# Cross-attention with prompts: value columns of the even batches moved from SyncE's DMA queue to GpSimd's and ScalarE's

## The chip, the cores and the metric

The kernel runs on one core of a Trainium2 chip. A core has TensorE (PE), VectorE (DVE), ScalarE (ACT) and GpSimd (POOL) for arithmetic. DMA transfers are issued in the instruction streams of SyncE (SP), ScalarE and GpSimd, and each stream is worked off in order. The metric is the device time of one execution in microseconds (us), the median of several runs; less is better.

## The reference

For each of 8 batches, 112 queries of 320 channels attend over 375 context tokens of 512 channels, with 20 heads of 16 channels. The last 4 tokens are image prompts with weights of their own; the other 371 are text.

```python
q, k_t, v_t = heads(hidden @ W_q), heads(text @ W_k), heads(text @ W_v)
probs_t  = softmax(q k_t^T * scale)                    # 112 x 371 for each head
text_out = probs_t @ v_t
qsem = l2norm(probs_t @ text)                          # 512 channels for each query and head
sem  = qsem @ l2norm(ip)^T                             # 4 prompts
probs_ip = softmax(q k_ip^T * scale + 0.5 * sem) * spatial_mask
out = (text_out + probs_ip @ v_ip) @ W_out + b_out + hidden
```

## The kernel before, in words

**One product for each head.** The norm of `probs_t @ text` needs only the Gram matrix of the text tokens. So the kernel multiplies the probabilities of each head with a tile `u`, whose columns are the Gram matrix of the context (symmetric, so only its upper part is held, in three chunks of 128 tokens), the prompts, a one for the sum of the probabilities, and the head's own 16 value columns. A product therefore gives the norm, the prompt similarities, the sum and the text output at once. It runs over 12 blocks of 32 tokens (`product`, L830 to L843). The 20 heads of a batch are taken as 5 groups of 4; the four heads of a group lie on four bands of 32 partitions and multiply side by side.

**How `u` comes about.** For each batch the Gram rows are computed by `gram` into `ug` and copied by 16 DMAs to the four bands of `u` (`gram_to_groups`, L543). The values are computed by `values` (L595) into `vext`: for even batches after the first, chunks 0 and 1 come from `two_chunks` (L644), whose last sums are made by GpSimd (L667), and chunk 2 is copied by ScalarE (L612). `values_to_dram` (L684) stores `vext` to a tile `vd` in DRAM, with the token bands in the order in which `u` holds them: four DMAs for chunks 0 and 1, two for chunk 2. `values_to_groups` (L704) loads it again into `vr` with the heads split over the four bands: four DMAs for each call, each to 32 partitions, in rows of 80 floats. `placed` (L751) then has GpSimd copy the 16 columns of each head of the next group from `vr` into `u`, one copy for each chunk (L755). There are two buffers of `u`, used by batches in turn; within a batch a copy must wait until PE has read the previous group's columns of that chunk.

**How the probabilities come.** PE multiplies queries and keys (L789), DVE takes the negated maximum (L802), ACT the exponential (L806), SyncE's DMAs place each head's probabilities in `xg` (L813), and DVE transposes them into the stationary operand of the product (L825). ACT also copies the prompt logits out of the score bank (L808).

**The order of the work is written out by hand.** Inside the main loop each engine's instructions stand in the order of the program. The loop takes the 40 steps (batch, group) in twos. `pair` (L1256) multiplies two groups against each other, interleaved with scores and probabilities of steps to come. In it, `placed` (L1275, L1288) has the second group's value columns put in; then comes `moved` (L1289), which issues transfers for the next batch; then pieces of `finish` (L1293 to L1295), the end of the previous batch, then `reduced` (L1296). `behind` (L1336) issues what PE does after a pair: projections, the Gram matrix and values of the next batch, and further pieces of `finish`.

**The finish of a batch** (`finish`, L907) is cut into pieces. GpSimd scales the prompt values (L973), adds them up (L976) and adds them to the attention (L980); PE turns the attention round (L985), ACT copies it (L989), and PE multiplies it with the output weights (L994).

**The stretch of the change.** For the odd batches b = 1, 3, 5 and the even batch nb = b + 1 after each, the program runs as follows. `behind` of group 1 has PE compute the values of chunks 0 and 1 of nb, and stores them. The pair of groups 2 and 3 of b follows; after the copies for group 3, `moved(b, 2)` loads chunks 0 and 1 of nb (L1334), and then `f(b - 1, 2)` issues the finish's piece with L973 to L980. `behind` of group 3 loads queries for later (L1443, issued by GpSimd at L178), computes chunk 2 of the values, turns the attention round (L985), stores chunk 2, makes keys (L563), runs the output product (L994), and moves the last Gram rows and the value columns of chunk 2 (L1451, L1452). The next pair is group 4 of b with group 0 of nb, which reads the new columns.

Of the kernel before, what the change touches and what calls it, by code (L numbers as in the profile page):

```python
# [20 lines left out]
def kernel(  # L21
# [14 lines left out]
    nc = tc.nc  # L36
# [6 lines left out]
    NT = (T + P - 1) // P  # L43
# [304 lines left out]
    def turned_inputs(bs, i0=0, i1=NC):  # L348

        t0, n = blocks_of(bs)  # L350
        if bs[0] not in inputs_turned:
            inputs_turned[bs[0]] = work.tile(
                [P, NC, 2 * S], F32, tag="xT", name=f"xT_{bs[0]}", bufs=1
            )
        xT = inputs_turned[bs[0]]
        nc.vector.transpose(
            xT[:, i0:i1, : n * RG].rearrange("p i (j r) -> p j i r", r=RG),
            x_in[:, :n, i0 * RG : i1 * RG].rearrange("p j (i c) -> p j i c", c=RG),
        )
# [53 lines left out]
    def load_next(b):  # L413
        if 2 <= b < B:
            loaded[b] = load_ctx(b)
# [127 lines left out]
    def gram_to_groups(b, blocks, eng=nc.sync):  # L543

        for q in blocks:
            for a in range(GROUP):
                eng.dma_start(
                    st[b]["u"][a * RG : (a + 1) * RG, q * GW : (q + 1) * GW],
                    ug[q * RG : (q + 1) * RG, :],
                )  # L550
# [133 lines left out]
    def values_to_dram(b, eng, c0=0, c1=NT):  # L684
        s = st[b]
        if b == 0:
            eng.dma_start(
                s["vd"][c0 * P : c1 * P].rearrange("(c p) x -> p c x", p=P),
                s["vext"][:, c0:c1, :C],
            )  # L690
            return
        for c in range(c0, c1):
            q = 0
            while q < QN:
                p, n = DEAL[c].index(q), 1
                while q + n < QN and p + n < QN and DEAL[c][p + n] == q + n:
                    n += 1
                to = c * P + p * RG
                eng.dma_start(
                    s["vd"][to : to + n * RG], s["vext"][q * RG : (q + n) * RG, c, :C]  # L700
                )
                q += n

    def values_to_groups(b, c0=0, c1=NT):  # L704
        s = st[b]
        w = NG * D
        for a in range(GROUP):
            nc.sync.dma_start(
                s["vr"][a * RG : (a + 1) * RG, c0 * QN : c1 * QN].rearrange(
                    "p j g d -> p j (g d)"  # L710
                ),
                s["vd"][c0 * P : c1 * P, a * w : (a + 1) * w].rearrange("(j i) x -> i j x", i=RG),
            )

    def prompt_values(b):

        nc.sync.dma_start(
            st[b]["vip"].rearrange("p n h d -> p (n h d)"),
            vipd[b * NIP : (b + 1) * NIP, :].rearrange("n c -> (n c)").partition_broadcast(S),
        )  # L720
# [94 lines left out]
    def transposed(b, g, j0=0, j1=BLK):  # L815

        xg = x_ring[(b * NG + g) % NX]
        if j1 < j0 + 1:
            return
        if ("xT", g) not in st[b]:  # L820
            st[b]["xT", g] = work.tile([P, BLK, P], F32, tag="xgT", name=f"xgT_{b}_{g}")
        xT = st[b]["xT", g]
        n = BLK // (2 if b == B - 1 or (b, g) == (0, 0) or j1 - j0 < BLK else 1)
        for j in range(j0, j1, n):
            nc.vector.transpose(  # L825
                xT[:, j : j + n].rearrange("p j (k q) -> p q j k", q=QN),
                xg[:, :, j * RG : (j + n) * RG].rearrange("p q (j k) -> p q j k", k=RG),
            )
# [379 lines left out]
    def f(b, pieces=1):  # L1208
        if b >= 0:
            run(("f", b), lambda: finish(b), pieces)  # L1210

    def k(b, pieces=1):
        run(("k", b), lambda: keys(b), pieces)

    def v(b, pieces=1):
        run(("v", b), lambda: values(b), pieces)

    def gr(b, pieces=1):
        run(("g", b), lambda: gram(b), pieces)
# [100 lines left out]
    def moved(b, g):  # L1320

        nb = b + 1
        if b % 2 == 0:
            if g in (1, 2):
                gram_to_groups(nb, (g - 1,))
            if g == 3:
                todo = [lambda: gram_to_groups(nb, (3,)), lambda: values_to_groups(nb)]
                for move in reversed(todo) if nb == B - 1 else todo:
                    move()
        else:  # L1330
            if g in (0, 1):
                gram_to_groups(nb, (g,))
            if g == 2:
                values_to_groups(nb, 0, 2)  # L1334

    def behind(n):  # L1336

        b, g = steps[n]
        nb = b + 1
        two = steps[n + 1 : min(n + 3, len(steps) - NG + 1)]  # L1340

        def tr(i):
            if i < len(two):
                transposed(*two[i], 0, BLK // (1 + i))

        if b % 2 == 0 and g == 0:
            if n == 0:
                turn[:] = ["sc", "sc", "mm"]
                turned_inputs(pairs[1])
            else:  # L1350
                turn[:] = ["qd"] * 4 + ["mm"]
                k(b)
                nc.scalar.preload_act_table(AF.Sqrt)
                f(b - 1)
                if b - 1 < B - 2:
                    prompt_values(b - 1)
            if n:
                token_sums(nb)
                gr(nb)
                tr(0)  # L1360
            if n:
                gr(nb, 2)
                f(b - 1)
            v(nb)
            if n == 0:
                k(nb)
                run(("pp",), prompt_projections)
            if n:
                tr(1)
                f(b - 1, 2)  # L1370
            load_next(b + 2)
        elif b % 2 == 0 and g == 2:
            turn[:] = ["qd"] * (8 if b else 3) + ["mm"]
            gram_to_groups(nb, (2,))
            if b == 0:
                run(("pp",), None)
                prompt_keys(nb)
                tr(0)
                v(nb)
                q(nb)  # L1380
                values_to_dram(nb, nc.scalar, 0, 2)
                v(nb)
                values_to_dram(nb, nc.scalar, 2)
                run(("pp",), None)
            else:
                values_to_dram(nb, nc.gpsimd, 2)
                k(nb)
                tr(0)
                v(nb)
                q(nb)  # L1390
                values_to_dram(nb, nc.gpsimd, 0, 2)
            tr(1)
        elif b % 2 == 0 and nb < B - 1:
            turn[:] = ["qd"] * (4 + (b > 0)) + ["mm", "mm"]
            turned(b + 2)
            token_sums(b + 2)
            q(nb)
            if b > 0:
                f(b - 1)
            else:  # L1400
                run(("t", b), lambda: prompt_logits(b))
            k(nb)
            tr(0)
            if b > 0:
                f(b - 1)
            gr(nb + 1, 3)
            if b > 0:
                f(b - 1)
            if n + 1 not in late:
                tr(1)  # L1410
            load_next(b + 3)
            f(b)
            prompt_values(b)
        elif b % 2 == 0:
            turn[:] = ["qd"] * 4 + ["mm"]
            q(nb, 2)
            f(b - 1)
            k(nb)
            nc.scalar.preload_act_table(AF.Sqrt)
            tr(0)  # L1420
            f(b - 1, 2)
            prompt_values(b)
            f(b, 2)
        elif g == 1:
            turn[:] = ["qd"] * 7 + ["sc", "mm", "mm"]
            gram_to_groups(nb, (2,))
            nc.scalar.preload_act_table(AF.Sqrt)
            q(b)
            k(b)
            f(b - 1)  # L1430
            nc.scalar.preload_act_table(AF.Exp)
            k(nb)
            tr(0)
            f(b - 1)
            v(nb)
            tr(1)
            f(b - 1)
            values_to_dram(nb, nc.sync, 0, 2)
            if b == B - 3:
                prompt_values_by_head()  # L1440
        else:
            turn[:] = ["qd"] * 3 + ["sc"]
            load_turned(nc.gpsimd, pairs[(b + 3) // 2])  # L1443
            v(nb)
            f(b - 1)
            values_to_dram(nb, nc.sync, 2)
            tr(0)
            k(nb)
            f(b - 1, 2)
            tr(1)  # L1450
            gram_to_groups(nb, (3,))  # L1451
            values_to_groups(nb, 2)  # L1452
        assert not turn, (b, g, turn)

    for n in range(0, len(steps) - NG, 2):
# [4 lines left out]
        b, g = steps[n]  # L1460
# [16 lines left out]
    b = B - 1  # L1477
# [125 lines left out]
```

## Time and profile before

| | |
|---|---|
| time, median of 3 runs | 407.21 us (406.81 to 408.14) |
| the profiled execution | 405.13 us |
| its span in the trace | 403.4 us |
| granted TensorE clock | 0.999 |
| busy PE, DVE, ACT, POOL | 398.0, 331.3, 198.5, 182.7 us |

The span is what the profiler saw of one execution, from the first instruction to the last; the execution took 1.7 us more. Times of the trace count from the start of the span. L755 is line 755 of the kernel. PEld is TensorE's weight load, which overlaps its matmuls (PE). "SPq" and "POOLq" are the sequencers that issue DMAs and wait for semaphores. In a name such as `u<-vr`, the left side is written and the right side is read. A timeline row gives start, length, engine, line, operation, shapes and count, and in brackets how long the engine had been idle and what released it; neighbouring instructions of one kind are merged. Matmuls are pipelined and their ends are modelled.

### The profile page before, as it was taken

The numbers are of one execution on the slowest core, as the hardware profiler recorded it, in microseconds if no ns is written. First come the engines' busy times: TensorE is split into PE (matmuls) and PEld (weight loads), VectorE is DVE, ScalarE is ACT, GpSimd is POOL, SyncE is SP. The second block draws the span as 40 slices with busy tenths as digits, with TensorE's granted clock in tenths as the row PEclk, the third lists the DMA queues.
The fourth block names the chain that finished last, engine by engine and source line by source line (L and its number), as shares of the span: only waits on it lengthen the run. The fifth ranks groups of instructions, "written<-read, shape, count | busy, mean of one in ns | idle before, by whom it ended". The sixth has DMA issues, their size and how long they took to land.

```text
span 403.4 us, 14380 instructions
## 1 busy us (share of the span) xinstructions
PE 398.0 (99%) x5673; PEld 321.9 (80%) x5673; DVE 331.3 (82%) x703; ACT 198.5 (49%) x707; POOL 182.7 (45%) x391
## 2 busy tenths in 40 slices
PE   8999999999999999999999999999999999999996
PEld 7867688888878787978787878877886878887894
DVE  3445789887998897987998898897798988888984
ACT  3146333337443943525653665334743485446764
POOL 7746021151571658051563338532256155704681
PEclk9999999999999999999999999999999999999999
DMA  7969846778666957567557766566746544776311
GB/s 228 215 186 225 189 130 179 207 190 184 166 172 166 220 130 185 148 161 166 155 157 165 199 165 171 160 171 152 187 126 174 131 124 117 195 172 174 107 52 28
DMA packets 58390, 65.85 MB, mean 163 GB/s; under 512 B 20165, under 2 KB 51641, under 8 KB 58324
## 3 DMA queue, kind: packets, MB, share of 16 engines
q1 hardware_dynamic: 54814, 58.23, 57.5%
q0 software_dynamic: 2336, 5.42, 5.4%
q10 hardware_dynamic: 1174, 1.29, 1.0%
q8 instruction: 45, 0.74, 0.9%
q14 instruction: 21, 0.17, 0.2%
HBM read 20.22 MB, written 5.22 MB: 63 GB/s over the span
## 4 chain that ended last, share of the span: by engine, by line
PE 97%; POOL 1%; DMA 1%; issue 0%; ACT 0%; SPq 0%; POOLq 0%
PE ps_qd L837 46%; PE ps_k L563 10%; PE ps_g L533 8%; PE ps_v L605 7%; PE ps_s L789 6%; PE ps_vs L663 6%; PE ps_q L394 3%; PE ps_o L994 3%; PE ps_k L580 3%; PE ps_g L495 1%; DMA ct<-in_ctx_dram 1%; PE ps_a L985 1%; PE ps_q L376 1%; PE ps_c L464 0%; POOL attn L980 0%; PE ps_o L1086 0%
## 5 line engine op out<-in xcount | busy, mean ns | idle before, releaser
L837 PE MATMUL ps_qd<-u,xgT 32*112 32x40 f32 (+11 forms) x3840 | 216.9, 352 | 0.2
L837 PEld LDWEIGHTS ps_qd<-u,xgT 32*112 32x112 f32 x3840 | 179.6, 172 | 32.0 <-issue 4.8
L825 DVE STREAM_TRANSPOSE xgT<-xg 128x768 f32<-128x768 f32 (+1 forms) x63 | 123.2, 1974 | 6.6 <-DMA xg<-p 5.9
L806 ACT ACTIVATE p<-ps_s,nmx 112x371 f32<-112x371 f32 x160 | 85.5, 585 | 63.2 <-DVE nmx L802 62.1
L802 DVE TENSOR_REDUCE nmx<-ps_s 112x1 f32<-112x371 f32 x160 | 76.7, 532 | 23.9 <-PE ps_s L789 22.5
L755 POOL COPY u<-vr 128x64 f32<-128x64 f32 x120 | 27.0, 237 | 152.4 <-PE ps_qd L837 82.8
L890 DVE CUSTOM_DVE_ANT_0 p<-ps_qd,p 112x371 f32<-112x371 f32 x152 | 73.5, 541 | 11.7 <-ACT pvs L864 7.4
L789 PE MATMUL ps_s<-kT,qm 32*112 32x375 f32 (+1 forms) x320 | 61.3, 485 | 0.0
L864 ACT COPY pvs<-ps_qd 112x21 f32<-112x21 f32 x152 | 21.8, 200 | 55.6 <-DVE ss L890 49.8
L563 PE MATMUL ps_k<-ctxT,wk_sb 128*128 128x371 f32 x128 | 43.4, 482 | 0.0
L563 PEld LDWEIGHTS ps_k<-ctxT,wk_sb 128*128 128x128 f32 x128 | 23.1, 190 | 12.8 <-issue 0.8
L533 PE MATMUL ps_g<-ctxT 128*32 128x119 f32 (+11 forms) x672 | 32.7, 338 | 0.0
L533 PEld LDWEIGHTS ps_g<-ctxT 128*32 128x32 f32 x672 | 27.7, 109 | 6.1 <-POOL xs L639 1.3
L789 PEld LDWEIGHTS ps_s<-kT,qm 32*112 32x112 f32 x320 | 27.6, 171 | 6.1 <-POOL vext L667 1.1
L605 PE MATMUL ps_v<-wv_sb,ctxT 128*128 128x320 f32 x96 | 28.3, 441 | 0.0
L452 DVE STREAM_TRANSPOSE ctxT<-ct 128x512 f32<-128x512 f32 x21 | 22.5, 1084 | 5.0 <-DMA u<-ug 5.0
L808 ACT COPY ipl<-ps_s 112x4 f32<-112x4 f32 x140 | 24.3, 174 | 0.0
L605 PEld LDWEIGHTS ps_v<-wv_sb,ctxT 128*128 128x128 f32 x96 | 17.5, 190 | 6.6
L570 ACT COPY kT<-ps_k 128x371 f32<-128x371 f32 x16 | 7.5, 469 | 23.1 <-PE ps_k L563 23.1
L973 POOL TENSOR_TENSOR vip<-vip,w 112x1280 f32<-112x1280 f32 (+1 forms) x8 | 17.5, 2185 | 0.2 <-DVE w L967 0.2
L517 POOL TENSOR_TENSOR ug<-ug,half 128x128 f32<-128x128 f32 (+1 forms) x24 | 10.6, 450 | 14.9 <-ACT ug L516 12.8
L512 ACT ACTIVATE ug<-ps_g 128x279 f32<-128x279 f32 (+5 forms) x24 | 8.0, 333 | 18.3 <-DMA ct<-in_ctx_dram 7.8
(179 smaller groups left out, 441.5 us busy)
## 6 DMA issues: line engine op xcount, KB each, us to landing
xg<-p SPq DMA_DIRECT2D x159, 162.3 KB
u<-ug SPq DMA_DIRECT2D x120, 99.0 KB
ct<-in_ctx_dram SPq DMA_DIRECT2D x28, 176.0 KB
vip<-vipd SPq DMA_DIRECT2D x7, 560.0 KB
vr<-vd SPq DMA_DIRECT2D x20, 120.0 KB
out_dram<-ob SPq DMA_DIRECT2D x7, 140.0 KB
vr<-vd SPq DMA_DIRECT2D x12, 80.0 KB
x_in<-in_x_dram POOLq DMA_DIRECT2D x12, 70.0 KB, 3.7
```

Of the source, the lines that this page charges most:

```text
L533: nc.tensor.matmul(ps[p * RG : (p + 1) * RG, s0 : T - t0], ctxT[:, e, t0 + q * RG : t0 + (q + 1) * RG], ctxT[:, e, t0 + s0 : T], start=(e ...
L563: nc.tensor.matmul(ps[:, :TT], wk_sb[:, e, i * P : (i + 1) * P], s["ctxT"][:, e, :TT], start=(e == 0), stop=(e == NE - 1),)
L605: nc.tensor.matmul(ps[:, :C], ctxT[:, e, c * P : (c + 1) * P], wv_sb[:, e, :], start=(e == 0), stop=(e == NE - 1),)
L663: nc.tensor.matmul(ps[:, :CH], a[:, k], t[:, k], start=(k == 0), stop=(k == 1))
L755: nc.gpsimd.tensor_copy(region(b, c)[:, :, UV - c * P :], s["vr"][:, c * QN : (c + 1) * QN, g, :])
L789: nc.tensor.matmul(ps[:S, :w], qm[a * RG : (a + 1) * RG, i, r, j * S : (j + 1) * S], s["kT"][a * RG : (a + 1) * RG, i, :w], start=True, st ...
L802: nc.vector.tensor_reduce(nmx, ps[:S, :TT], AX.X, ALU.max, negate=True)
L806: nc.scalar.activation(p, ps[:S, :TT], AF.Exp, bias=nmx)
L808: nc.scalar.copy(s["ipl"][:, groups[g][a], :], ps[:S, TT:T])
L825: nc.vector.transpose(xT[:, j : j + n].rearrange("p j (k q) -> p q j k", q=QN), xg[:, :, j * RG : (j + n) * RG].rearrange("p q (j k) -> p ...
L837: nc.tensor.matmul(banks[a][:S, j * RG : UW], xT[a * RG : (a + 1) * RG, j, :S], region(b, c)[a * RG : (a + 1) * RG, p, q * RG :], start=(j ...
L890: nc.vector.tensor_tensor_reduce(out=p, in0=ps[:S, :TT], in1=p, scale=1.0, scalar=0.0, op0=ALU.mult, op1=ALU.add, accum_out=s["ss"][:, h : ...
```

## The change

For the even batches 2, 4 and 6, four groups of transfers go by other queues:

- the stores of chunks 0 and 1 to DRAM: GpSimd in place of SyncE;
- the loads of chunks 0 and 1 into `vr`, issued by `moved`: GpSimd in place of SyncE;
- the store of chunk 2: ScalarE in place of SyncE;
- the loads of chunk 2: GpSimd in place of SyncE, and in the program ahead of the last Gram rows, which stay on SyncE.

The transfers themselves, their sizes and the data are the same. Batches 0, 1, 3, 5 and 7 are as they were.

```diff
-    def values_to_groups(b, c0=0, c1=NT):
+    def values_to_groups(b, c0=0, c1=NT, eng=nc.sync):
         s = st[b]
         w = NG * D
         for a in range(GROUP):
-            nc.sync.dma_start(
+            eng.dma_start(
...
             if g == 2:
-                values_to_groups(nb, 0, 2)
+                values_to_groups(nb, 0, 2, nc.gpsimd)
...
             f(b - 1)
-            values_to_dram(nb, nc.sync, 0, 2)
+            values_to_dram(nb, nc.gpsimd, 0, 2)
             if b == B - 3:
                 prompt_values_by_head()
...
             v(nb)
             f(b - 1)
-            values_to_dram(nb, nc.sync, 2)
+            values_to_dram(nb, nc.scalar, 2)
             tr(0)
             k(nb)
             f(b - 1, 2)
             tr(1)
+            values_to_groups(nb, 2, NT, nc.gpsimd)
             gram_to_groups(nb, (3,))
-            values_to_groups(nb, 2)
```

## The prediction

> **What bounds the kernel now.** I read the page first, for which engine the end hangs on, then the chain in order of time, for whether that engine ever waits near the lines of the change, and then the timelines of the engines that get the moved transfers. From the page: the granted clock in 40 slices, the chain by engine, and one group.
>
> ```profile
> PEclk9999999999999999999999999999999999999999
> ...
> PE 97%; POOL 1%; DMA 1%; issue 0%; ACT 0%; SPq 0%; POOLq 0%
> ...
> L825 DVE STREAM_TRANSPOSE xgT<-xg 128x768 f32<-128x768 f32 (+1 forms) x63 | 123.2, 1974 | 6.6 <-DMA xg<-p 5.9
> ```
>
> TensorE (PE) is 97% of the chain, at full clock in every slice. So time comes off only where PE itself waits, and whatever makes PE wait goes on the end in full, because no later idle stretch takes it up again. The whole case is then: which PE waits sit beside SyncE's transfers of the value columns, and does the new place of those transfers make PE wait?
>
> The chain in order of time (start, length, what) round the second of the three even batches that change, and the same stretch of the third:
>
> ```profile
> 209.59 2.35 PE ps_v L605 x8
> 211.95 0.29 PE ps_a L985 x3
> 212.24 2.51 PE ps_k L563 x8
> 214.75 1.61 PE ps_o L994 x6
> 216.36 1.15 PE ps_qd L837 x10
> ...
> 227.06 1.40 PE ps_k L580 x15
> ...
> 311.37 1.15 PE ps_qd L837 x10
> ...
> 322.60 0.46 PE ps_k L580 x3
> ```
>
> From 209.59 to 216.36 each piece begins where the one before ended: no gap. The product pair that follows takes 227.06 - 216.36 = 10.70 us here and 322.60 - 311.37 = 11.23 us in the third batch: 0.53 us lost there. That is what late SyncE placements cost: the weight load that sat idle in that pair is this one (PE weight loads, timeline; the bracket is idle time and its releaser).
>
> ```profile
> 317.19 1.83 PEld L837 LDWEIGHTS ps_qd<-u,xgT 32*112 32x112 f32 x34 [0.26 <-ACT ipl L808]
> ```
>
> It waited for a bank that ScalarE (ACT) empties after the scores, and ScalarE was late behind VectorE, whose transposes (L825) are on the page with 5.9 us of waiting for xg<-p. Relieving SyncE can give back this 0.53 us and little more; in the second batch the pair lost nothing.
>
> **What GpSimd is doing there.** GpSimd (POOL), timeline, second batch, contiguous rows:
>
> ```profile
> 199.47 1.50 POOL L667 TENSOR_TENSOR vext<-vext,v 128x160 f32<-128x160 f32 x3
> 202.14 0.24 POOL L755 COPY u<-vr 128x64 f32<-128x64 f32 x1 [1.17 <-PE ps_qd L837]
> 203.60 0.24 POOL L755 COPY u<-vr 128x64 f32<-128x64 f32 x1 [1.22 <-PE ps_qd L837]
> 205.14 0.25 POOL L755 COPY u<-vr 128x64 f32<-128x64 f32 x1 [1.30 <-PE ps_qd L837]
> 205.38 2.47 POOL L973 TENSOR_TENSOR vip<-vip,w 112x1280 f32<-112x1280 f32 x1
> 207.92 1.54 POOL L976 TENSOR_TENSOR vip<-vip 112x640 f32<-112x640 f32 x1
> 209.54 1.81 POOL L980 TENSOR_TENSOR attn<-attn,vip 112x320 f32<-112x320 f32 x2
> 211.29 0.59 POOL L755 COPY u<-vr 128x64 f32<-128x64 f32 x3
> 211.81 2.41 POOL L178 DMA_DIRECT2D x_in<-in_x_dram  x4
> ```
>
> The weight load of the attention transposes, PE, same batch:
>
> ```profile
> 211.51 0.51 PEld L985 LDWEIGHTS ps_a<-ident,attn 112*128 112x128 f32 x3
> ```
>
> These rows carry the forecast. From the copy at 205.14 on, GpSimd works without a pause through L973, L976 and L980; L980 ends at 209.54 + 1.81 = 211.35, and the weight load that reads its result begins at 211.51. GpSimd's part of the finish is just in time, and PE's matmul (211.95) follows at once. The first and the last of the three batches look the same:
>
> ```profile
> 114.39 1.81 POOL L980 TENSOR_TENSOR attn<-attn,vip 112x320 f32<-112x320 f32 x2
> ```
> ```profile
> 116.40 0.51 PEld L985 LDWEIGHTS ps_a<-ident,attn 112*128 112x128 f32 x3
> ```
> ```profile
> 304.55 1.81 POOL L980 TENSOR_TENSOR attn<-attn,vip 112x320 f32<-112x320 f32 x2
> ```
> ```profile
> 306.52 0.51 PEld L985 LDWEIGHTS ps_a<-ident,attn 112*128 112x128 f32 x3
> ```
>
> 116.20 against 116.40, and 306.36 against 306.52. In the code, moved(b, 2) stands between placed() (L1288, the copy at 205.14) and f(b-1, 2) (L1295, which issues L973 to L980). The change puts four loads on GpSimd exactly there.
>
> **The change, part by part.** Prices first: GpSimd's stores of this tile and their landing, and its loads of x_in, which are four transfers of 32 partitions in rows of 320 bytes like the moved loads (duration min/median/max in ns).
>
> ```profile
> L699 POOL DMA_DIRECT2D vd<-vext x18: 502/529/590, 153.2 to 351.6; - x18
> ...
> DMA to landing us min/median/max: 2.5/3.1/3.8
> ```
> ```profile
> L178 POOL DMA_DIRECT2D x_in<-in_x_dram x16: 548/592/668, 30.7 to 308.5; - x16
> ```
>
> 1. Four stores (chunks 0 and 1) go from SyncE to GpSimd (L1438). They follow the end of vext, 199.47 + 1.50 = 200.97, and take 4 x 0.53 = 2.1 us, to 203.1. The copy of 202.14 is behind them and slips by 1.0 us, to end at 203.3. The cover: PE still has the rest of one group's blocks to do, since it releases the copy of the next chunk only at 203.60 and reads the first copy after that. So I price it at 0; without the cover it would be at most 1.0 us a batch.
>
> 2. Four loads of chunks 0 and 1 go to GpSimd (L1334), behind the copy that ends at 205.39. First they wait for the stores to land. The last store is issued at 202.55; 3.1 us later is 205.7, a wait of 0.3 us. The ends: 0 (landing in 2.5), and 1.5 us if 3.8 us count from the end of its issue (203.1 + 3.8 = 206.9). I take 0.3, the median. Then 4 x 0.60 = 2.4 us of issue (ends: 4 x 0.53 = 2.1 and 4 x 0.67 = 2.7). So L973 starts 2.7 us late, and L980 ends 2.7 us late, at about 214.05.
>
> 3. What PE loses: its weight load waits for L980, and behind it on PE, in a fixed order, stand the key projection (212.24) and the output projection (214.75), so nothing fills the hole. The spare time is between 0.16 us (weight load at 211.51) and 0.60 us (matmul at 211.95, both against 211.35); a weight load and its latency go between, so I take 0.4. Stall 2.7 - 0.4 = **2.3 us a batch**, three batches: 6.9 us. By the ends: 2.1 + 0 - 0.6 = 1.5 and 2.7 + 1.5 - 0.16 = 4.0, or 4.5 to 12 us in all.
>
> 4. Two stores of chunk 2 go to ScalarE (L1446). ScalarE, timeline:
>
> ```profile
> 212.31 0.45 ACT L989 COPY aT<-ps_a 128x336 f32<-128x336 f32 x1
> 214.78 0.47 ACT L570 COPY kT<-ps_k 128x371 f32<-128x371 f32 x1 [2.03 <-PE ps_k L563]
> ```
>
> They go into 2.03 us of idle time, and SyncE issues the same two in 1.16 us (below): 0. Both neighbours slip with PE, so the cover stays; without it, 1.2 us a batch.
>
> 5. Four loads of chunk 2 go to GpSimd and ahead of the Gram rows (L1451, L1452). They stand behind L178, then wait for ScalarE's stores. How long such stores take is bounded by SyncE's, timeline of its queue:
>
> ```profile
> 213.59 1.16 SPq L699 DMA_DIRECT2D vd<-vext  x2
> 214.81 2.49 SPq L547 DMA_DIRECT2D u<-ug  x4
> 217.82 1.74 SPq L708 DMA_DIRECT2D vr<-vd  x4
> ```
>
> Issued by 214.75, and the loads that wait for them go out at 217.82: 3.1 us at most. On PE's shifted clock (2.3 us later) ScalarE's stores end near 216.1, land by 219.2, and the four loads are out by 219.2 + 2.2 = 221.4. Queued behind them are the copies for the next batch's first group, done by 221.9. PE starts the pair at 216.36 + 2.3 = 218.7 and reads those copies only once the first group's ten leading blocks are through: forty matmuls, of which the ten of 216.36 take 0.115 us each, so some 4.6 us (later blocks are narrower, but eight score matmuls lie between): 223.3. Spare 1.4 us: 0, and without that cover up to 1 us a batch.
>
> 6. SyncE loses 14 transfers a batch and places xg<-p sooner: the 0.53 us comes back, and I count it whole.
>
> **Sum.** 6.9 - 0.53 = 6.4 us. The profiled execution of before took 405.13 us (span 403.4, so 1.7 us round it): 411.5. The median of before is 407.21, 2.1 us above that execution, so the forecast is **413.6 us**, 1.6% slower.
>
> **One rule that speaks against the change.** GpSimd's 18 stores took 502 to 590 ns with VectorE busy beside them. The Trainium skill, SBUF — State Buffer, section "SBUF: two separate sides", says that descriptors of GpSimd's DMAs can't be written while VectorE holds the shared port in certain fast modes, and gives about 620 ns alone against 3100 ns overlapped. By that figure, as an estimate, the four loads would cost 12.4 us and the change some 37 us. The trace doesn't agree: no issue here exceeds 0.67 us.
>
> **Rivals.**
> - *The loads don't hold GpSimd's arithmetic* (an issue is handed off and L973 runs on): only item 6 is left, 407.21 - 0.5 = 406.7 us, not slower. It decides if L973 still starts at about 205.4. For it: transfers run beside arithmetic. Against: on the timeline GpSimd's own row for L178 is busy 2.41 us for four issues. Chance 0.07, most of it within 0.3%.
> - *The wait for the landing is the larger part*: 1.5 us in place of 0.3, so 3.5 us a batch, 10.5 - 0.5 = 10: 417 us. For it: a landing of up to 3.8 us. Inside the range; chance 0.12.
> - *Each load is held until a VectorE instruction ends*, 1.97 us (L825) in place of 0.60: 5.5 us more a batch, so 413.6 + 16.5 = 430 us. Against it the 668 ns above. Chance 0.03. This is the port rule of the Trainium skill at this kernel's own durations.
> - *The hole lets PE's clock drop*: if a hole of 2 to 4 us halves the clock for the next pieces (2.51 + 1.61 us), each batch pays 4.1 us more: 413.6 + 12.4 = 426 us. For it: this trace has no hole that long amid dense work. Against: the granted clock is 9 in all slices. Chance 0.05. The Trainium skill, TensorE: Matmul & The Clock Gate, section "What's actually happening", puts the idle window at about 3.4 us, above my 2.3.
>
> **How the numbers follow.** The forecast's own case has 0.73, with the long landing 0.85. The bounds of the unknown costs run from 4.5 - 0.5 = 4 us (411.2) to 12 - 0.5 = 11.5 (418.7); the three runs of before lie 0.4 us below to 0.9 us above their median, so I put 0.5 us round them: 410.7 to 419.3. Left out: 0.15. About 0.3% (1.2 us) is what a measurement of this kernel can tell from no change; slower by more than that 0.93, within it 0.05, faster 0.02 (PE has no more than 0.6 us to give here).
>
> **What would show it.** In the changed profile: four DMA rows for vr<-vd on GpSimd between the third L755 copy and L973; L973 starting some 2.7 us after that copy; PE's weight load of ps_a (L985) waiting for attn L980 three times, 2 to 2.5 us each; the pair after it at 10.7 us in all three batches. I am wrong if L985 shows no wait, if PE waits for L755 copies instead (items 1 and 5), or if the granted clock shows a slice under 9.

## The result, and the profile after

The changed kernel took 418.0 us (median of 6 runs, 415.97 to 421.4); the kernel before took 407.15 us in runs beside it. The medians lie 10.8 us apart. The ratio that the runs of both give is 1.0301 (95% interval 1.0266 to 1.0335), or about 12.3 us (10.8 to 13.6), and the text goes by it: slower, as forecast, but by nearly twice the forecast 6.4 us. The profiled execution, 420.88 us with a span of 419.2, is one of the longer ones; its parts are 15.8 us above the span of before.

The page of the changed kernel, the same parts as were shown of before: granted clock in 40 slices, and the chain by engine.

```profile
PEclk9999999999989999999997999999998999999998
...
PE 85%; POOL 8%; issue 2%; DMA 2%; DVE 1%; ACT 1%; POOLq 0%; DVEq 0%
```

PE has gone from 97% to 85% of the chain, and GpSimd has 8%. And the clock, which stood at 9 in every slice of before, falls in three places in the body of the run: slices 12, 22 and 31, where the three even batches are made ready. (In the last slice the kernel ends.)

GpSimd's timeline, second batch, in answer to the nine rows of before:

```profile
205.54 2.09 POOL L699 DMA_DIRECT2D vd<-vext  x4
207.62 0.25 POOL L755 COPY u<-vr 128x64 f32<-128x64 f32 x1
208.21 0.24 POOL L755 COPY u<-vr 128x64 f32<-128x64 f32 x1 [0.33 <-PE ps_qd L837]
209.75 0.25 POOL L755 COPY u<-vr 128x64 f32<-128x64 f32 x1 [1.30 <-PE ps_qd L837]
211.56 2.33 POOL L708 DMA_DIRECT2D vr<-vd  x4 [1.57 <-DMA vd<-vext]
213.91 2.48 POOL L973 TENSOR_TENSOR vip<-vip,w 112x1280 f32<-112x1280 f32 x1
216.46 1.54 POOL L976 TENSOR_TENSOR vip<-vip 112x640 f32<-112x640 f32 x1
218.08 1.81 POOL L980 TENSOR_TENSOR attn<-attn,vip 112x320 f32<-112x320 f32 x2
```

The stores run where they were expected, the four loads stand between the third copy and L973, and ahead of them GpSimd sits 1.57 us until the stores have landed. L973 starts 213.91 - 210.00 = 3.9 us after the third copy's end; before it followed at once.

PE's timeline, first the kernel before (second batch: the value projection and the attention transposes), then the changed kernel, second and first batch:

```profile
209.53 2.42 PE L605 MATMUL ps_v<-wv_sb,ctxT 128*128 128x320 f32 x8
211.78 0.45 PE L985 MATMUL ps_a<-ident,attn 112*128 112x112 f32 x3
```
```profile
214.13 2.42 PE L605 MATMUL ps_v<-wv_sb,ctxT 128*128 128x320 f32 x8
219.95 0.82 PE L985 MATMUL ps_a<-ident,attn 112*128 112x112 f32 x3 [3.39 <-POOL attn L980]
```
```profile
114.87 2.42 PE L605 MATMUL ps_v<-wv_sb,ctxT 128*128 128x320 f32 x8
119.64 0.76 PE L985 MATMUL ps_a<-ident,attn 112*128 112x112 f32 x3 [2.35 <-POOL attn L980]
```

From the start of one to the start of the other it was 2.25 us and is now 5.82 and 4.77: holes of 3.6 and 2.5 us. The third batch:

```profile
315.51 2.42 PE L605 MATMUL ps_v<-wv_sb,ctxT 128*128 128x320 f32 x8
320.13 0.51 PE L985 MATMUL ps_a<-ident,attn 112*128 112x112 f32 x3 [2.19 <-POOL attn L980]
```

That is 4.62, a hole of 2.4 us. Together 8.5 us. (The brackets are PE's own idle time, a little less, since the tail of the value projection runs into the hole.)

That is not all. The chain in order of time, changed kernel: the transposes and the key projection behind them in each batch, and for the third batch the pair that follows, with its end:

```profile
119.64 0.76 PE ps_a L985 x3
120.40 3.94 PE ps_k L563 x8
...
219.95 0.82 PE ps_a L985 x3
220.77 4.95 PE ps_k L563 x8
...
320.13 0.51 PE ps_a L985 x3
320.63 4.20 PE ps_k L563 x8
324.83 1.61 PE ps_o L994 x6
326.45 1.15 PE ps_qd L837 x10
...
337.15 1.40 PE ps_k L580 x14
```

The key projection (ps_k, x8) took 2.51 us before. Now it takes 3.94, 4.95 and 4.20 us, with the same matmuls and nothing to wait for: 5.6 us more. The granted clock shows why. In windows of 0.1 us it stands at 0.50 from 119.75 to 123.16, from 218.74 to 225.56 and from 321.14 to 324.55, and at 1.00 in the rest of the body. These stretches are 3.41, 6.82 and 3.41 us long, and their starts lie 98.99 and 102.40 us apart: 29 and 30 times 3.413. So in this execution the clock changes only on a fixed grid of 3.41 us. These are the windows of that grid round the holes (window and length; PE, weight loads, VectorE, ScalarE, GpSimd busy; then the granted clock, the DMA share and GB/s):

```profile
116.34:119.75 3.41, 1.06 (x5) 0.47 (x4) 3.41 (x10) 0.67 (x5) 3.25 (x5) 1.00 0.70 197
119.75:123.16 3.41, 3.41 (x8) 2.15 (x9) 1.44 (x1) 0.44 (x1) 2.74 (x7) 0.50 0.79 206
...
215.32:218.74 3.42, 1.24 (x5) 0.57 (x3) 3.42 (x10) 0.83 (x7) 3.26 (x3) 1.00 0.69 189
218.74:222.15 3.41, 2.20 (x6) 1.64 (x7) 1.57 (x1) 0.44 (x1) 3.33 (x8) 0.50 0.63 151
222.15:225.56 3.41, 3.41 (x7) 1.69 (x7) 0.00 (x0) 0.00 (x0) 2.05 (x5) 0.50 0.42 114
225.56:228.98 3.42, 3.42 (x31) 2.02 (x33) 1.54 (x2) 0.47 (x1) 2.12 (x6) 1.00 0.39 74
...
317.72:321.14 3.42, 1.23 (x7) 0.77 (x7) 3.42 (x7) 0.86 (x2) 3.26 (x8) 1.00 0.76 199
321.14:324.55 3.41, 3.41 (x7) 1.92 (x6) 0.60 (x1) 0.00 (x0) 1.60 (x3) 0.50 0.58 156
```

Each fall comes at the end of a window in which PE had been idle for 2.2 to 2.4 us, be the hole over by then (the first and the third) or not (the second). The clock comes back at the end of the next window in which PE was busy throughout. In the second batch the hole ran 1.2 us into the next window, and there the clock stayed low for a window more. So each hole is paid for twice: once while PE waits, and once while it works slowly behind it. PE worked for some 12.4 us at half speed (3.41, 5.6 and 3.41), which is 6.2 us lost; 5.6 us of it show in the key projections, most of the rest in the transposes.

The sum of the profiled execution: 8.5 us of holes and 5.6 us of slow key projections, less the 0.53 us that the pair after the third batch gets back (337.15 - 326.45 = 10.70, from 11.23), is 13.5 of the 15.8 us. The rest is in pieces of about a microsecond or less, in the transposes themselves (0.76 and 0.82 us in place of 0.29, in part by the clock), in the pair ahead of the first hole and behind the chain's last instruction; I made no experiment on it.

### The profile page after: what moved, and what is told of

The parts are those of the page before. It is cut to its first block, busy times and chain, and to the rows that moved or that the text cites. A ratio compares the mean times of both kernels' runs of the same rounds, so it can differ in the third digit from the quotient of the medians.

```text
span 419.2 us, 14370 instructions
## 1 busy us (share of the span) xinstructions
PE 404.6 (97%) x5673; PEld 324.7 (77%) x5673; DVE 331.4 (79%) x703; ACT 198.8 (47%) x707; POOL 202.4 (48%) x427
## 4 chain that ended last, share of the span: by engine, by line
PE 85%; POOL 8%; issue 2%; DMA 2%; DVE 1%; ACT 1%; POOLq 0%; DVEq 0%
PE ps_qd L837 39%; PE ps_k L563 11%; PE ps_g L533 8%; PE ps_s L789 6%; PE ps_v L605 5%; PE ps_vs L663 5%; PE ps_q L394 3%; PE ps_o L994 3%; PE ps_k L580 2%; POOL vip L973 2%; POOL attn L980 2%; POOL vip L976 1%; PE ps_g L495 1%; POOL vr L708 1%; DMA vd<-vext 1%
## 5 line engine op out<-in xcount | busy, mean ns | idle before, releaser
L837 PE MATMUL ps_qd<-u,xgT 32*112 32x232 f32 (+11 forms) x3840 | 216.6, 352 | 0.2
L563 PE MATMUL ps_k<-ctxT,wk_sb 128*128 128x371 f32 x128 | 49.1, 532 | 0.0
L563 PEld LDWEIGHTS ps_k<-ctxT,wk_sb 128*128 128x128 f32 x128 | 25.8, 211 | 15.2 <-issue 5.0
L708 POOL DMA_DIRECT2D vr<-vd x24 | 13.5, 571 | 9.4 <-DMA vd<-vext 8.6
L517 POOL TENSOR_TENSOR ug<-ug,half 128x128 f32<-128x128 f32 (+1 forms) x24 | 10.7, 447 | 14.7 <-ACT ug L516 12.3
L973 POOL TENSOR_TENSOR vip<-vip,w 112x1280 f32<-112x1280 f32 (+1 forms) x8 | 17.5, 2185 | 0.3 <-DVE w L967 0.2
```

The lines of the kernel that those rows point to most:

```text
L563: nc.tensor.matmul(ps[:, :TT], wk_sb[:, e, i * P : (i + 1) * P], s["ctxT"][:, e, :TT], start=(e == 0), stop=(e == NE - 1),)
L837: nc.tensor.matmul(banks[a][:S, j * RG : UW], xT[a * RG : (a + 1) * RG, j, :S], region(b, c)[a * RG : (a + 1) * RG, p, q * RG :], start=(j ...
L973: eng.tensor_tensor(wv[:, some], wv[:, some], by[:, some], ALU.mult)
```

## The experiments

Theory A: the four loads of chunks 0 and 1, by their place in GpSimd's queue ahead of L973, make the holes, and the holes lower the clock. Theory B: moving fourteen transfers to other queues costs by itself, through delayed copies and colliding transfers, and the clock falls for reasons of its own.

**Put the four loads back on SyncE.** The edit to the changed kernel:

```diff
             if g == 2:
-                values_to_groups(nb, 0, 2, nc.gpsimd)
+                values_to_groups(nb, 0, 2)
```

> The change, with the four loads of chunks 0 and 1 put back on SyncE; everything else stays on GpSimd and ScalarE. Theory A (these four loads stand in GpSimd's queue ahead of L973, make the hole at ps_a, and the hole lowers the clock): the whole loss goes; no wait of ps_a for attn L980 in the three batches beyond the 0.4 us of the last batch, clock 0.999, ps_k behind it 2.5 us each, 406.5 to 407.7 us. Theory B (the loss comes from GpSimd's and ScalarE's queues as a whole: stores that delay the copies, transfers that collide): most of the 11 to 13 us stays, 414 us or more.

Measured: 405.88 us (12 runs) beside 407.22, ratio 0.998 (0.9959 to 1.0), clock 0.997 in the profiled execution. PE's wait for the attention is left only in the last batch, where it was before:

```profile
PE ps_a L985 <- POOL attn L980: 0.2, 1, 0.2
```

The whole loss has gone with these four loads; it ended a little below the 406.5 to 407.7 us that A named. Theory B falls: stores on GpSimd, stores on ScalarE and the chunk-2 loads on GpSimd are all still there.

**Move nothing but these four loads.** The edit to the kernel before: the new argument `eng`, and

```diff
             if g == 2:
-                values_to_groups(nb, 0, 2)
+                values_to_groups(nb, 0, 2, nc.gpsimd)
```

> The kernel before, with nothing moved but the four loads of chunks 0 and 1, to GpSimd ahead of L973; their stores stay on SyncE. Theory A: these four alone make the loss. Their wait for SyncE's stores is a little longer (issued up to 1 us later than GpSimd's), so holes of 3.2 to 3.7 us and a lower clock behind each: 418 to 424 us. Theory B (the sum of all moves is what costs): 410 us or less.

Measured: 418.27 us, ratio 1.0275 (1.0207 to 1.0343), as much as the whole change within the intervals. PE's timeline of its profile, the transposes and the key projection (whose length on the timeline is 2.67 us at full clock), first batch and second batch:

```profile
121.37 0.51 PE L985 MATMUL ps_a<-ident,attn 112*128 112x112 f32 x3 [2.51 <-POOL attn L980]
121.71 2.67 PE L563 MATMUL ps_k<-ctxT,wk_sb 128*128 128x371 f32 x8
```
```profile
218.86 0.51 PE L985 MATMUL ps_a<-ident,attn 112*128 112x112 f32 x3 [2.26 <-POOL attn L980]
219.20 4.36 PE L563 MATMUL ps_k<-ctxT,wk_sb 128*128 128x371 f32 x8
```

In the first batch PE was idle for 2.51 us ahead of the transposes and the clock held; in the second it was idle for 2.26 us and the clock fell, and in the third (2.24 us) it fell too. The holes are shorter than the 3.2 to 3.7 us that A named. And the length of a hole alone doesn't decide it: its place on the grid does. In this execution the clock stood at 0.50 from 219.53 to 222.94 and from 318.52 to 321.93, again 3.41 us each and 29 times 3.413 apart. The same grid counted back to the first batch cuts its hole in two:

```profile
117.13:120.54 3.41, 1.73 (x7) 0.91 (x5) 3.41 (x10) 1.46 (x9) 3.18 (x4) 1.00 0.60 167
120.54:123.96 3.42, 2.59 (x11) 1.74 (x12) 2.24 (x1) 0.44 (x1) 3.42 (x8) 1.00 0.71 178
...
216.12:219.53 3.41, 1.15 (x6) 0.55 (x5) 3.41 (x9) 0.55 (x2) 3.25 (x7) 1.00 0.59 165
219.53:222.94 3.41, 3.41 (x7) 2.00 (x6) 0.87 (x1) 0.31 (x1) 2.18 (x4) 0.50 0.75 185
...
315.10:318.52 3.42, 1.18 (x7) 0.67 (x6) 1.61 (x8) 0.43 (x1) 3.26 (x7) 1.00 0.82 196
```

The hole of 2.51 us gave 1.7 us of idle PE to one window and 0.8 to the next, and the clock held. The others lay whole in one window and gave it 2.2 to 2.3 us, and the clock fell at its end.

**Keep the loads on GpSimd, but behind the finish.**

```diff
         if g in (1, 2):
             f(b - 1, 2)
+        if b % 2 and g == 2:
+            values_to_groups(b + 1, 0, 2, nc.gpsimd)
...
-            if g == 2:
-                values_to_groups(nb, 0, 2, nc.gpsimd)
```

> The change, with the four loads of chunks 0 and 1 still on GpSimd but issued behind L980 instead of ahead of L973. Theory A: position is all that counts; the copies for the next group slip by about 2.4 us into their spare 4.5 us, no hole at ps_a, clock 0.999, and the 0.5 us of late placements is gained: 406.2 to 407.2 us. Theory B (transfers on GpSimd's queue cost PE time wherever they stand, and the chunk-2 loads then come late for the copies of the next batch): 410 us or more, with PE waiting for L755.

Measured: 408.38 us, ratio 1.0029 (1.0007 to 1.0051). Position is nearly all, but the run is over 1 us above what A gave. GpSimd's timeline in the first batch shows a second wait that comes to light once the hole is gone:

```profile
125.12 2.19 POOL L708 DMA_DIRECT2D vr<-vd  x4 [2.30 <-DMA vd<-vext]
127.31 0.41 POOL L755 COPY u<-vr 128x64 f32<-128x64 f32 x2
```

The chunk-2 loads wait for ScalarE's stores, the copies of the next batch stand behind them, and PE's weight loads wait for such copies (0.4 us in all before; total, times, longest):

```profile
PEld ps_qd L837 <- POOL u L755: 1.3, 4, 0.6
```

**Give PE other work in the hole.** The key projection goes ahead of the transposes:

```diff
+            k(nb)
             f(b - 1)
             values_to_dram(nb, nc.scalar, 2)
             tr(0)
-            k(nb)
             f(b - 1, 2)
```

> The change, with PE's key projection (2.51 us) ahead of the attention transposes, so that PE has work in the hole. Theory A: the hole shrinks from 2.4 to 3.4 us to below 1, a short wait for ScalarE's copy aT (about 0.6 us) comes in ahead of ps_o, the clock stays at 0.999: 1 to 4 us above the kernel before, 408 to 411 us. Theory B (clock drops and delays do not hang on the hole): 415 us or more, with clock 0.98 to 0.99.

Measured: 411.3 us, ratio 1.0102 (1.0074 to 1.013), clock 0.997 to 0.999 in every run. The hole is filled but for 0.6 us in the second batch, the clock holds, and two thirds of the loss go. What is left stands in the main in PE's waits: for ScalarE's copy, now directly ahead of the output product, and again for copies into u.

```profile
PE ps_o L994 <- ACT aT L989: 1.7, 3, 0.6
PE ps_qd L837 <- POOL u L755: 1.5, 1, 1.5
```

**Keep PE busy in the hole with work of no use.** Dummy matmuls, 24 and then, in a second run, 11, ahead of the transposes:

```diff
         ps = bank(f"ps_a_{b}", spare=True)
+        if b in (0, 2, 4):
+            for _ in range(24):
+                nc.tensor.matmul(ps[:, :P], ident, ident, start=True, stop=True)
```

> The change, with 24 matmuls of the identity (128 columns) put ahead of the attention transposes of the three batches, into the bank that the transposes overwrite: they add work and take nothing away. Theory A (the hole itself lowers the clock): PE is busy in most of the hole, the clock stays at 0.999, ps_k behind it takes 2.5 us in place of 3.9 to 5.0, while the hole's own length stays: 3 to 6 us less than the change, 412 to 415 us. Rival (the clock drops for another reason, such as power or the run): no gain, 417 us or more, ps_k still 4 to 5 us.

Measured with 24: 422.15 us, ratio 1.0367 (1.0333 to 1.04), clock 0.998. The clock held, but the gain that A named didn't come, since 24 of these take 5.36 us and outlast the hole: a mistake in the size of the experiment. So again with 11:

> As the run with 24 dummy matmuls, with 11 of them: those 24 took 5.36 us, 0.223 each, and so outlasted the hole; 11 take 2.46 us, less than the mean hole of the change. They add work and take nothing away. Theory A (the hole lowers the clock, and the clock's part of the loss is 1.4 + 2.4 + 1.7 = 5.6 us in the change's profile): clock 0.999, ps_k 2.5 us after all three holes, total 411 to 414 us, 4 to 6 below the change. Rival (the clock drops for another reason): 417 us or more.

Measured: 414.64 us, ratio 1.0198 (1.0144 to 1.0251), clock 0.996 to 0.999 in its four runs (0.981 to 0.993 in the six of the change); the time is a little above the 411 to 414 us that A named. The chain in the first batch (each dummy shows as two rows):

```profile
116.83 2.46 PE ps_a L986 x22
119.29 0.32 PE ps_a L988 x3
119.61 2.51 PE ps_k L563 x8
```

The transposes still wait out the hole, but behind it the key projection is back at 2.51 us, and so in the other two batches. The time, 8.0 us above before by the ratio (5.8 to 10.2), is what the holes cost without the clock. The rest of the change's 12.3, about 4.2 us a run, is the clock; by the intervals of the two ratios that size is known only to within some 2.6 us. The granted clocks fit it: they average 0.987 over the change's six runs against 0.999, which is 1.2% of the time: an estimate of 5 us, from which the part that fell into idle time goes off.

**Take the wait for landing out.** The loads read the batch before, so that the text columns of batches 2, 4 and 6 come from other tokens; once with four loads on GpSimd (the edit shown), once with two there and two on SyncE (the last argument is then 2):

```diff
-    def values_to_groups(b, c0=0, c1=NT, eng=nc.sync):
+    def values_to_groups(b, c0=0, c1=NT, eng=nc.sync, src=None, few=GROUP):
...
-            eng.dma_start(
+            (eng if a < few else nc.sync).dma_start(
...
-                s["vd"][c0 * P : c1 * P, a * w : (a + 1) * w].rearrange("(j i) x -> i j x", i=RG),
+                (src or s)["vd"][c0 * P : c1 * P, a * w : (a + 1) * w].rearrange("(j i) x -> i j x", i=RG),
...
-                values_to_groups(nb, 0, 2, nc.gpsimd)
+                values_to_groups(nb, 0, 2, nc.gpsimd, st[b], 4)
```

> The change, but the four loads of chunks 0 and 1 on GpSimd read the stored values of the batch before, which landed long ago: same shapes and issues, no wait for landing (the text columns of batches 2, 4 and 6 are then of other tokens). Theory A: the issues alone hold L973 back by 2.3 to 2.5 us, hole 1.8 to 2.1 us a batch in place of 2.4 to 3.9; 411.5 to 413 us if a hole of 2 us leaves the clock at 0.999, 414 to 417 if not. Rival (the landing wait is nearly all of the cost): 409 us or less.

> As the run without the landing wait, but only two of the four loads on GpSimd, the other two on SyncE, all reading the batch before (text columns of batches 2, 4 and 6 of other tokens). Theory A: L973 1.2 us late, hole 0.6 to 0.9 us a batch, clock 0.999: 408 to 410 us. Rival (a load costs a fixed hole whatever the number, by the switch of GpSimd to a transfer): as with four loads, 411 us or more.

Measured: 413.42 us, ratio 1.0168 (1.0113 to 1.0224), and 409.77 us, ratio 1.0069 (1.0038 to 1.01). PE's waits for the attention, four times each run, with 0.2 us of the last batch in the sum; four loads, then two:

```profile
PE ps_a L985 <- POOL attn L980: 5.8, 4, 1.9
```
```profile
PE ps_a L985 <- POOL attn L980: 2.3, 4, 0.8
```

GpSimd's two issues in the second of these, second batch:

```profile
207.74 1.18 POOL L708 DMA_DIRECT2D vr<-vd  x2
```

The price goes by the number of loads. In both profiles the key projection is at 2.51 us in all three batches: idle times up to 1.95 us did not lower the clock there, of which at most 1.80 us lay in one window of the grid (counted back from the clock's fall at the end of the run, 409.15). With four loads, though, two of the four runs had clocks of 0.992 and 0.994, so it probably fell there; these two have no trace.

**Two smaller versions.** Only the two stores of chunk 2 moved to ScalarE, in the kernel before:

```diff
-            values_to_dram(nb, nc.sync, 2)
+            values_to_dram(nb, nc.scalar, 2)
```

> The kernel before with one thing moved: the two stores of chunk 2 on ScalarE. Theory A (all that SyncE's relief can give is the 0.5 us lost in one of the three pairs): 406.5 to 407.3 us, ratio 0.998 to 1.0. Rival (ScalarE's stores land later, 4.3 us after their issue in the change's first batch against 2.9 for SyncE's, and hold up the next batch's copies): 1.001 to 1.004.

Measured: 406.92 us, ratio 1.0012 (0.999 to 1.0035): no difference that this can tell, and not A's gain.

All stores as in the change, all loads on SyncE in their old places:

```diff
-                values_to_groups(nb, 0, 2, nc.gpsimd)
+                values_to_groups(nb, 0, 2)
...
-            values_to_groups(nb, 2, NT, nc.gpsimd)
             gram_to_groups(nb, (3,))
+            values_to_groups(nb, 2)
```

> The change's stores (chunks 0 and 1 on GpSimd, chunk 2 on ScalarE) with all loads on SyncE in their old places. Theory A (the stores cost nothing, the loads were the cost): 406 to 407.3 us, ratio 0.997 to 1.0, ps_a without a wait in the three batches. Rival (GpSimd's stores, 2.1 us ahead of the copies, cost PE time): 1.002 or more, PE waiting for L755 in the pairs of groups 2 and 3.

Measured: 405.01 us beside 405.82, ratio 0.9973 (0.9947 to 1.0). That is 1.1 us below before, with an interval that ends at no change; with only the four loads put back it was 0.8 us, and the two can't be told apart. The stores on GpSimd cost PE nothing that shows.

## Why the prediction was right and wrong

- *PE is the bound, and a wait of PE goes on the end in full.* Right; the holes of the profile and the holes by the 11 dummies (8.5 - 0.5 us, and 8.0 us) agree within the interval.
- *Item 1, the stores on GpSimd: 0.* Right. In the second batch they delayed the first copy to 207.62, and the next still came at 208.21, on PE's release.
- *Item 2, L973 is 2.7 us late.* Right in two batches, short in one. The four issues took 2.33 us (2.4 foretold). The wait ahead of them was priced at 0.3; it was 0.4 in the first and the third batch, where L973 came 2.8 and 2.7 us after the third copy, and 1.57 in the second, where it came 3.9 us after it. There the stores took 3.9 us to land from the end of their issue (207.63 to 211.56), past the 3.8 us of the stated end.
- *Item 3, PE loses 2.3 us a batch.* Measured 2.5, 3.6 and 2.4: 8.5 us in place of 6.9. So this term was 1.6 us short, most of it by the landing in the second batch.
- *Items 4 and 5, chunk 2: 0.* Right on the whole, by luck. ScalarE's stores were thought to land within 3.1 us. In the change's first batch GpSimd's loads came much later than that after their issue:

```profile
120.50 1.15 ACTq L699 DMA_DIRECT2D vd<-vext  x2
```
```profile
126.34 2.19 POOL L708 DMA_DIRECT2D vr<-vd  x4 [3.85 <-DMA vd<-vext]
```

  From the end of the stores at 121.65 to 126.34 are 4.7 us; in the other two batches it was 2.2 and 2.7. The slow key projection held PE back too, and so hid it; with the loads behind the finish it may be what cost about a microsecond.
- *Item 6, 0.53 us comes back.* Right: the third pair took 10.70 us. The run with the four loads back on SyncE is 0.8 us below before, with an interval that reaches no change.
- *The clock.* This is the step that failed. The sum counted the hole alone and put the slow work behind it at nothing; the rival with a clock that drops got a chance of 0.05, on the ground that the clock of before never fell. But that trace has no hole of such length amid the work, so it could not bear on it. The rival's mechanism held. Its size, 4.1 us a batch, was too large, since it halved the clock for the key and the output projection in every batch; what ran slowly was PE's work in one window of 3.41 us, or two: 1.4, 2.4 and 1.7 us in the profiled execution's key projections, about 4.2 us a run in all. Holes of 8.0 us and a clock of 4.2 us give the 12.3 us.
- *The range.* The 418.0 us lie inside 410.7 to 419.3, but by luck: the upper end was reached with long landings and no spare time in every batch, and no slow clock is in it.
- *The rule against the change.* The conclusion held: the issues that GpSimd took over needed 0.50 to 0.61 us each. But "no issue here exceeds 0.67 us" is not so: the trace of before has GpSimd issues of other, larger transfers at 0.73 us (x_sb, mean of three) and 0.79 us (wo_sb).

The Trainium skill, TensorE: Matmul & The Clock Gate, section "What's actually happening", puts the state with half the clock behind an idle window of about 3.4 us. The half agrees (0.50 in the windows above), and so does the length of the window (3.41 us between changes). As a safe length for a hole the 3.4 us do not hold here: the clock fell with 2.2 to 2.4 us of idle PE in one window. The prediction set that figure against its 2.3 us as a point that spoke against the rival.

What decides whether a hole of 2 to 2.5 us lowers the clock was read from the traces afterwards; no run was made to test it. In the body of the kept traces, every window with 2.17 us or more of idle PE was followed by a fall (five, in two executions), and none with 1.80 us or less was. The limit lies between, in this work. It is not idle time alone: at the very end of the kernel, amid short single matmuls, the clock fell behind a window with 1.6 us of idle PE (the run with the four loads back on SyncE). And the grid stood otherwise in the two executions, so a hole of this length can be cheap in one and dear in the next; that may be why the change's clocks spread from 0.981 to 0.993, which no trace shows.

## What to carry to other kernels

When a transfer is moved to another engine's queue, look up which instruction stands next in that queue and who waits for it: the same stores moved in front of work with time to spare cost nothing, and four loads in front of work that was just in time cost 12 us. A load that depends on a store brings the store's landing with it, and the engine that issues it waits that out. And where TensorE is busy throughout, price a new hole of two microseconds or more twice, once as waiting and once as slow work behind it: here half of each window of 3.41 us that ran at half clock, so 1.7 us or, with two windows, 2.8.

## What the runs showed of the hardware that was not expected

- The granted clock fell to 0.50 at or up to 1.0 us behind holes with 2.2 to 3.4 us of idle PE, and the key projection behind took 3.9 to 5.0 us in place of 2.51. It fell and rose only on a grid of 3.41 us, for one or two windows (3.41 or 6.82 us). With PE kept busy by 11 useless matmuls it stayed at 0.996 to 0.999, and the kernel was faster for doing more: a ratio of 1.0198 to before, against 1.0301.
- GpSimd took 2.33 us for four load issues of 32 partitions with VectorE busy beside it all the time; two took 1.18. No sign of an issue held back by VectorE.
- Stores to DRAM that ScalarE issued let the dependent loads start 4.7 us after their issue ended in the change's first batch and 2.2 and 2.7 us in the other two; with the loads of chunks 0 and 1 back on SyncE it was 5.1, 4.5 and 3.9 us. With these stores and their loads on SyncE it had been 2.6 to 3.1 us.
